# Steps that make the gather lists stand at other places in TensorE's work on x's chunks

## The chip, the cores and the metric

The kernel runs on one core of one Trainium2 chip. The metric is the device time of an execution in microseconds (us); lower is better. A core has five engines with a queue each: PE (TensorE, matmuls), DVE (VectorE), ACT (ScalarE), POOL (GpSimd) and SP (SyncE, which only issues DMAs here). Each works through its own instructions in the order of the program; they wait for each other on semaphores.

## The reference

`x` is 8 x 2048 x 128, `adj` a sparse 2048 x 2048 matrix (each entry is drawn with probability 0.002, made symmetric, and the diagonal is always there). Two layers follow each other:

```python
# layer 0
sj = inputs @ w_j
si = inputs @ w_i
res = si[:, :, None] + sj[:, None, :] + relation[None] * w_r + g_b
agg = jnp.einsum('bij,bjd->bid', res, inputs)
x = _layernorm(x + agg @ weight + bias, axis=-1)
# layer 1, A1 = A2 = adj
x1 = jnp.einsum('bnf,nw->bwf', x0, A)
x2 = 2.0 * jnp.einsum('bnf,nw->bwf', x1, A) - x0
out = jax.nn.relu(concat([X, x1, x2, x1, x2]) @ Theta1 + bias)
x = _layernorm(x + out, axis=-1)
```

The dense terms of layer 0 (si, sj) are of low rank. What costs is the product with `adj`, once in layer 0 and in two hops in layer 1.

## The kernel before, in words

The 2048 rows are 16 chunks of 128; a row of all eight batches has 1024 numbers. Four target chunks of layer 0 (0 to 3) are multiplied densely with adj's transposed columns. The other twelve, and both hops, use lists: for a strip of 32, 64 or 128 columns of `adj` the kernel finds the rows that have a nonzero there, gathers the adj entries of these rows and the rows of y (or u) by indirect DMAs from POOL's queue, and multiplies the small blocks.

The work before layer 0 runs in three stages.

1. `R_ORDER` loop: the chunks of `adj` are loaded and transposed, DVE reduces them to masks (which strip has a nonzero in which row), and the first eight chunks of x are done on the way. The transposed chunks are stored to `rr_d`, later joined there by copies of adj's columns (twelve DMAs of 1 MB on SP, `copies`).
2. The loop `for n in range(NX, NC)` over the remaining eight chunks of x (block n below). A block has eight transposes (`x_t`, PE, into banks 6 and 7, copied by ACT), the projections y = x W with si and sj (`y_of`, PE into banks 4 and 5, copied by ACT), and the dense pairs: `full_rows(0, acc0, ...)` and `full_rows(1, acc1, ...)`, two matmuls of 128x512 each (four instructions a pair in the trace), for target chunks 0 and 1. Between these stand the steps that make the lists, called by `lists_at`.
3. The code after the loop, written out by hand: more rounds for the lists, jobs, column sums, the dense target chunks 0 to 3, and then a loop over chunks 4 to 15 of layer 0.

The list chain goes through PE, ACT and DVE in turns. It makes first the lists of the 32-wide strips ("T"), then those of the halves ("H": 64- and 128-wide strips, which take the columns that are shared).

- `ranked`: a matmul with a triangle of ones into bank 6 ranks the rows of a column; DVE marks the first 64 in `et`.
- `candidates`: 14 transposing matmuls of `et` into banks 6 and 7, copied to `cand` by ACT. Then eight `round_of` on DVE: `max` takes the eight largest, `match_replace` strikes them out.
- `lists_end(0)`: turns the T lists (matmuls into bank 6, six DVE operations) into row numbers `idx`, `idr` and the flag `has`.
- `encode2`, `split2`, `candidates2`: the same for the halves: DVE encodes into `e2`, PE ranks into bank 7, DVE splits, PE transposes nine blocks into banks 6 and 7, ACT copies to `cand2`.
- `rounds2([r])`: round r of eight on `cand2` (96 x 1152). `lists_end(1)`, after the rounds, gives idx, idr and has for the halves.

A job fetches adj entries: `get_job` issues four (T) or three (H) indirect DMAs from `rr_d` into one of four slots of `st`; `keep_job` (DVE) multiplies what came with `has` and puts it into `rct` and `rc`, which frees the slot. `next_job` is a keep_job and a get_job. There are 24 jobs. `get_direct` gathers the adj entries of chunks 0 to 3 directly (28 DMAs). `get_rows` gathers rows of y.

The engines' instructions are kept in the order of the calls (class `Tied`), but the indirect DMAs of POOL's queue are placed by the scheduler: some gathers stand earlier than the calls do. Before, the queue has eight jobs (32 gathers), the memset of `rc`, six direct gathers, two y gathers (into `ring` and `trp`), and then direct gathers, jobs and y gathers mixed. The first gather of rows for chunk 4 into `Y` is the 93rd gather of the queue.

Before the loop's end nothing of DVE is between `split2` and `rounds2([0])`. After `rounds2([0])` comes a memset of banks 4 and 5, and then the first `next_job`.

```python
    rounds2([0])
    for b in bank[4:6]:
        dve.memset(b, 0.0)
    next_job()
    rounds2([1, 2])
    next_job()
```

All recorded operations have the line of a helper (L74), so that groups and instructions are told apart by the tiles.

Of the kernel before, what the change touches and what calls it, by code (L numbers as in the profile page):

```python
# [11 lines left out]
ALU = mybir.AluOpType  # L12
AX = mybir.AxisListType
# [5 lines left out]
def kernel(  # L19
# [44 lines left out]
    X_ORDER = list(range(ND, NC)) + list(range(ND))  # L64
# [11 lines left out]
    pe, dve, act = Tied(nc.tensor), Tied(nc.vector), Tied(nc.scalar)  # L76
# [47 lines left out]
    def load_later_constants():  # L124
        for i in range(4):
            sp.dma_start(out=b0row[:, i, :], in_=bias0[None, :])
        sp.dma_start(out=b1bc[:, 0, :], in_=bias1[None, :].to_broadcast([P, D]))
        sp.dma_start(out=th, in_=theta.rearrange("(m p) f -> p m f", p=P))
# [61 lines left out]
    both = st[:, 2 * NC * NT + 512:2 * NC * NT + 768].rearrange("p (c w) -> p c w", w=NC)  # L190
# [7 lines left out]
    def at_of(c):  # L198
        t = at4[:, c] if c < ND else ats[(c - ND) % len(ats)]
        return t.rearrange("p (j i) -> p j i", i=P)  # L200
# [17 lines left out]
    def load_x(c, t):  # L218
        sp.dma_start(out=t, in_=x[:, c * P:(c + 1) * P, :].rearrange("b p f -> p b f"))
        return t  # L220

    def copies(cs):
        for c in cs:
            sp.dma_start(out=rr_d[c - ND][:, 1, :], in_=adj[:, c * P:(c + 1) * P])
# [4 lines left out]
    def pump():  # L229
        while todo:  # L230
            what, n = todo[0]
            if what == "a" and n < done["a"] + 3:
                for w in (slice(0, N // 2), slice(N // 2, N)):
                    sp.dma_start(
                        out=am[n % 3][:, w], in_=adj[R_ORDER[n] * P:(R_ORDER[n] + 1) * P, w]
                    )
            elif what == "x" and n < done["x"] + 6:
                c = X_ORDER[n]
                xin[c] = load_x(c, ring[:, X_SLOT[n % 6]])
                if c < ND:  # L240
                    zs[c] = xin[c]
            elif what == "k":
                load_later_constants()
            elif what == "s" and done["a"] == NC:
                store_rt(n)
            elif what == "c" and done["a"] == NC:
                copies([n])
            else:
                return
            todo.pop(0)  # L250
# [31 lines left out]
    def store_rt(c):  # L282
        sp.dma_start(out=rr_d[c - ND][:, 0, :].rearrange("(j p) i -> p j i", p=P), in_=at_of(c))
# [11 lines left out]
    def y_of(n, xt):  # L295
        for b in range(0, B, 2):
            py = bank[4 + b // 2 % 2][:, 0:2 * (D + 2)].rearrange("p (i f) -> p i f", i=2)
            for i in range(2):
                pe.matmul(py[:, i, :], xt[b // HB][:, (b + i) % HB, :], wx, start=True, stop=True)
            act.copy(Y[:, X_ORDER[n], b:b + 2, :], py[:, :, 0:D])  # L300
            act.copy(sraw[:, X_ORDER[n], b:b + 2, :], py[:, :, D:D + 2])
# [14 lines left out]
    def half(c, h):  # L316
        return Y[:, c, h * HB:(h + 1) * HB, :].rearrange("p b f -> p (b f)")
# [13 lines left out]
    def full_rows(c, accs, js):  # L331
        at = at_of(c)
        for j in js:
            for h in range(2):
                pe.matmul(
                    accs[h], at[:, j, :], half(j, h), start=(j == js_first[c]), stop=False,
                    skip_group_check=True,
                )
# [3 lines left out]
    def acc_pair():  # L342
        par[0] ^= 1
        return bank[2 * par[0]:2 * par[0] + 2]

    acc0, acc1 = acc_pair(), acc_pair()
# [21 lines left out]
    def thetas():  # L368
        dve.tensor_add(th[:, 4, :], th[:, 2, :], th[:, 4, :])
        dve.tensor_sub(th[:, 2, :], th[:, 0, :], th[:, 4, :])  # L370
        dve.tensor_add(th[:, 0, :], th[:, 4, :], th[:, 4, :])
        dve.tensor_add(th[:, 1, :], th[:, 1, :], th[:, 3, :])
# [18 lines left out]
    miss = const.tile([P, 3], F32)  # L391
# [27 lines left out]
    def ranked():  # L419

        b = bank[6][:, 0:2 * NT].rearrange("p (r t) -> p r t", r=2)
        pe.matmul(b, lt, sums, start=True, stop=True)
        before = b
        for c in range(LR):
            dve.tensor_add(etr[:, :, c, :], before, mt[:, :, c, :])
            before = etr[:, :, c, :]
        dve.scalar_tensor_tensor(et, et, 64.0, NS_[:, 0:LT, :], op0=ALU.is_le, op1=ALU.mult)
# [5 lines left out]
    def encode2():  # L433
        dve.tensor_sub(NS_[:, 0:LT, :], NS_[:, 0:LT, :], et)
        nsp = NS_.rearrange("p c (w i) -> p c w i", i=2)
        dve.tensor_mul(pr, pr, num[:, :, None].to_broadcast([P, NC, 2 * NC]))
        dve.tensor_add(pr, pr, nsp[:, :, :, 0])
        for to, c in (
            (e2[:, 0:LR, 0:HC], slice(0, LR)), (vm, slice(LT, NC)),
            (e2[:, NP - LR:, HC:], slice(LR, LT)),  # L440
        ):
            n = c.stop - c.start
            dve.tensor_add(to[:, :, 0:32], pr[:, c, :], nsp[:, c, :, 1])
            dve.tensor_mul(
                to[:, :, 32:HC], both[:, c, :], num[:, c, None].to_broadcast([P, n, NC])
            )
        dve.tensor_scalar(mm, vm, 0.0, None, op0=ALU.is_gt)
        dve.tensor_scalar(m2, e2[:, 0:LR, 0:HC], 0.0, None, op0=ALU.is_gt)
        dve.tensor_reduce(ms[:, 0, :], m2.rearrange("p c l -> p l c"), AX.X, ALU.add)
        dve.tensor_add(ms[:, 1, :], ms[:, 0, :], mm[:, 0, :])  # L450
# [8 lines left out]
    def candidates():  # L459
        for g in range(0, LR, 4):  # L460
            b = by4(bank[6 + g // 4])
            n = min(4, LR - g)
            for i in range(n):
                for r in range(2):
                    pe.matmul(
                        b[64 * r:64 * r + 64, i, :], et[:, r * LR + g + i, :], ident, start=True,
                        stop=True, skip_group_check=True, tile_position=(0, 64 * r),
                    )
            act.copy(cand[:, g * P:(g + n) * P].rearrange("p (i f) -> p i f", f=P), b[:, 0:n, :])
# [14 lines left out]
    def round_of(to, of, r):  # L484
        dve.max(to[:, 8 * r:8 * r + 8], of)
        if r < 7:
            dve.match_replace(of, to[:, 8 * r:8 * r + 8], of, 0.0)
# [47 lines left out]
    def gather(to, src, ids, n, rows):  # L535
        pool.indirect_dma_start(
            out=to, out_offset=None, in_=src,
            in_offset=bass.IndirectOffsetOnAxis(ap=ids[:, n:n + 1], axis=0),
            bounds_check=rows - 1, oob_is_err=False,
        )  # L540

    def columns(c, what):
        if what == "T":
            return [QT * c + t for t in range(QT)]
        return [NT + 2 * c, NT + 2 * c + 1, NT + 2 * NC + c]
# [7 lines left out]
    def staged(k):  # L553
        return st[:, k % 4 * BD:]

    def get_job():
        what, c = jobs[got[0]]
        s = staged(got[0])
        got[0] += 1
        for n, i in enumerate(columns(c, what)):  # L560
            gather(
                s[:, n * 2 * P:(n + 1) * 2 * P], rr_d[c - ND].rearrange("n m f -> n (m f)"), idx, i,
                N,
            )
# [148 lines left out]
    def rounds2(rs):  # L713
        for r in rs:
            round_of(lists2[0:96], cand2[0:96], r)

    def next_job():
        keep_job()
        get_job()


    def lists_at(n):
        if n == 9:
            ranked()
        if n == 10:
            candidates()
            for r in range(8):
                round_of(lists, cand, r)
            dve.tensor_reduce(miss[:, 1:2], both, AX.XY, ALU.add)
            thetas()  # L730
        if n == 13:
            lists_end(0)
            get_job()
            get_job()
            encode2()
            get_job()
            get_job()
        if n == 14:
            split2()
        if n == 15:  # L740
            candidates2()

    for n in range(NX, NC):
        xt = x_t(n)
        pump()
        y_of(n, xt)
        lists_at(n)
        for c, acc in enumerate((acc0, acc1)):
            full_rows(c, acc, [X_ORDER[n - 1]])
        if n % 4 == 0:  # L750
            s_rows(X_ORDER[n - 4])
        if n == 9:
            s_rows(X_ORDER[0])
# [80 lines left out]
        load_own(0, y0_d, c, Y[:, c] if c < 12 else ring[:, 3 + c % 2], c < 12)  # L834


    rounds2([0])
    for b in bank[4:6]:
        dve.memset(b, 0.0)
    next_job()  # L840
    rounds2([1, 2])
    next_job()
    for c0 in range(0, NC, 4):
        column_sums(c0)
    make_ub()
    rounds2([3, 4])
    next_job()
    si_t(0)
    si_t(1)
# [327 lines left out]
```

## Time and profile before

| | us |
|---|---|
| median of 3 runs | 826.9 |
| lowest and highest of them | 826.63, 828.11 |
| the profiled execution, whole | 869.73 |
| its span, first to last instruction | 867.5 |
| PE busy | 734.0 (85%) |
| POOL busy | 444.1 (51%) |
| DVE busy | 396.4 (46%) |
| ACT busy | 195.0 (22%) |

The profile is of one execution, which took longer than the timed ones; its mean granted TensorE clock is 0.940 of full speed. Times in the profile count from the span's start. A line of the timeline has the start, the duration, the engine, the operation with the tile that it writes and those that it reads, and in brackets how long the engine idled before it and what ended that. A POOL line DMA_INDIRECT is one gather. In the profile `y_d` stands also for `y0_d`, buffer numbers being left out.

### The profile page before, as it was taken

The page shows a single profiled execution, that of the slowest core. Times are in us where ns is not written, and L with a number is a line of the kernel's source. Part 1 is how long each engine was busy: PE and PEld are TensorE (multiplying, and loading weights), DVE is VectorE, ACT ScalarE, POOL GpSimd, SP SyncE. Part 2 cuts the span into 40 slices and gives each one's busy share as a digit, 9 for nine tenths or more (in the row PEclk, how much of TensorE's full clock was granted, in tenths as well). Part 3 has the DMA queues.
Part 4 walks back from the last instruction along what each step waited for, and adds up shares of the span by engine and source line. Part 5 has one row for each costly group of instructions (what it writes and reads, how often), then busy time and mean ns, then how long its engine had stood idle before and what let it go on. Part 6 is the DMA issues. An engine that isn't in the chain of part 4 may idle for free.

```text
span 867.5 us, 10065 instructions
## 1 busy us (share of the span) xinstructions
PE 734.0 (85%) x3534; PEld 369.1 (43%) x3534; DVE 396.4 (46%) x603; ACT 195.0 (22%) x440; POOL 444.1 (51%) x433
## 2 busy tenths in 40 slices
PE   5988999679830869879999889999999889999993
PEld 4665666524420323434444534334343344444441
DVE  6675758093500506547664300000000267777775
ACT  5675544212310002223333200000000011111111
POOL 1000001556777574766662556665665567777640
PEclk9999999797975798889999999999999999999997
DMA  8999999992233455898997989999999689999982
GB/s 308 291 326 332 294 306 298 359 379 60 87 110 98 133 162 166 278 358 316 380 371 265 376 289 359 370 359 359 354 364 349 217 304 343 348 377 386 389 284 62
DMA packets 167059, 250.87 MB, mean 289 GB/s; under 512 B 17480, under 2 KB 118557, under 8 KB 167000
## 3 DMA queue, kind: packets, MB, share of 16 engines
q0 software_dynamic: 49280, 145.59, 47.1%
q1 hardware_dynamic: 95736, 79.31, 29.1%
q10 hardware_dynamic: 21984, 25.24, 8.2%
q8 instruction: 30, 0.49, 0.2%
q14 instruction: 29, 0.24, 0.1%
HBM read 231.67 MB, written 58.72 MB: 335 GB/s over the span
## 4 chain that ended last, share of the span: by engine, by line
PE 53%; DMA 22%; issue 9%; ACT 6%; another core or an unknown queue 6%; POOL 2%; DVE 1%; POOLq 0%; ACTq 0%
PE bank L74 53%; DMA Y<-u_d,idx 11%; DMA Y<-y_d,idx 5%; ACT Y L74 2%; POOL Y L74 2%; DMA ring<-y_d,idx 2%; ACT trp L74 1%; ACT rct L74 1%; DMA trp<-y_d,idx 1%; DMA y_d<-st 1%; DMA ring<-in_x_dram 1%; DVE st L74 1%; DMA wr<-in_L_gnn_g_w_dram 1%; ACT at L74 1%
## 5 line engine op out<-in xcount | busy, mean ns | idle before, releaser
L74 POOL DMA_INDIRECT Y<-y_d,idx x170 | 185.0, 1088 | 105.4 <-PE bank L74 51.4
L74 PE MATMUL bank<-Y,rc 128*32 128x512 f32 (+2 forms) x896 | 220.1, 609 | 20.0 <-DMA Y<-u_d,idx 9.0
L74 POOL DMA_INDIRECT st<-rr_d,idx x84 | 85.8, 1021 | 189.6 <-DVE rown L74 144.4
L74 POOL DMA_INDIRECT Y<-u_d,idx x112 | 111.6, 997 | 82.9 <-issue 45.1
L74 PEld LDWEIGHTS bank<-Y,rc 128*32 128x32 f32 (+2 forms) x896 | 58.0, 128 | 178.0 <-issue 121.3
L74 PE MATMUL bank<-Y,at 128*128 128x512 f32 x256 | 116.5, 606 | 0.0
L74 DVE TENSOR_REDUCE s<-sq 128x4 f32<-128x512 f32 x60 | 41.1, 686 | 71.8 <-ACT sq L74 47.3
L74 PEld LDWEIGHTS bank<-Y,at 128*128 128x128 f32 x256 | 48.3, 195 | 54.0 <-issue 53.8
L74 PE MATMUL bank<-th,at 128*128 128x128 f32 x384 | 52.3, 291 | 14.3 <-issue 14.1
L74 DVE COPY ring<-bank 128x512 f32<-128x512 f32 x10 | 6.9, 692 | 115.3 <-PE bank L74 74.9
L74 PEld LDWEIGHTS bank<-th,at 128*128 128x128 f32 x384 | 48.7, 203 | 20.1 <-issue 19.7
L74 PE MATMUL bank<-ident,rc 128*128 128x128 f32 (+2 forms) x302 | 46.1, 302 | 12.1 <-DMA rc<-in_adj_dram 6.4
L74 ACT COPY ring<-bank 128x512 f32<-128x512 f32 (+1 forms) x36 | 20.8, 585 | 156.2 <-PE bank L74 90.0
L74 PE MATMUL bank<-ub,sit 5*128 5x512 f32 x16 | 8.4, 1053 | 49.0 <-ACT sit L74 40.6
L74 DVE TENSOR_REDUCE st<-rc 128x64 f32<-128x2048 f32 x16 | 36.5, 2282 | 24.7 <-DMA rc<-in_adj_dram 24.7
L74 PE MATMUL bank<-wx,trp 128*128 128x130 f32 x256 | 37.6, 290 | 10.7 <-ACT sraw L74 5.0
L74 PE MATMUL bank<-Y,rct 128*32 128x512 f32 (+1 forms) x232 | 45.8, 607 | 0.7 <-DMA Y<-y_d,idx 0.6
L74 PEld LDWEIGHTS bank<-ident,rc 128*128 128x128 f32 (+2 forms) x302 | 34.9, 155 | 25.2 <-issue 9.5
L74 PE MATMUL bank<-ring,rd 128*128 128x512 f32 x92 | 43.5, 594 | 1.2 <-issue 1.2
L74 ACT ACTIVATE sq<-ring 128x512 f32<-128x512 f32 x26 | 16.4, 630 | 121.1 <-DVE ring L74 96.5
L74 PEld LDWEIGHTS bank<-wx,trp 128*128 128x128 f32 x256 | 31.9, 194 | 16.0 <-ACT sraw L74 8.4
L74 ACT COPY trp<-bank 128x512 f32<-128x512 f32 (+1 forms) x38 | 21.2, 586 | 62.0 <-PE bank L74 59.6
(173 smaller groups left out, 890.7 us busy)
## 6 DMA issues: line engine op xcount, KB each, us to landing
rc<-in_adj_dram SPq DMA_DIRECT2D x32, 512.0 KB
rr_d<-in_adj_dram SPq DMA_DIRECT2D x12, 1024.0 KB
ring<-in_x_dram SPq DMA_DIRECT2D x16, 512.0 KB
rr_d<-Y SPq DMA_DIRECT2D x8, 1024.0 KB
y_d<-Y SPq DMA_DIRECT2D x16, 512.0 KB
u_d<-ring ACTq DMA_DIRECT2D x12, 512.0 KB
ring<-u_d SPq DMA_DIRECT2D x10, 512.0 KB
y_d<-ring ACTq DMA_DIRECT2D x10, 512.0 KB
```

The costliest lines, as they stand in the source:

```text
L74: return lambda *a, **k: tc.keep_in_program_order(f(*a, **k))
```

## The change

`lists_at` gets a second argument and is called three times in a block: ahead of the projections (step 0), between them and the first dense pair (step 1), and between the two pairs (step 2). The steps move so:

- `ranked`: from block 9 after the projections to block 9 before them.
- `candidates` and its eight rounds: from block 10 after the projections to block 9 between the pairs.
- `lists_end(0)`, four jobs and `encode2`: from block 13 after the projections to block 12 after them. The reduction of `both` into `miss` and `thetas` (five small DVE operations) move from behind the eight rounds to behind `encode2`.
- `split2`: from block 14 to block 13, after the projections.
- `candidates2`: from block 15 after the projections to block 13 between the pairs.
- Round 0 of the halves' lists stands in block 14, rounds 1 and 2 in block 15. After the loop, round 3 stands between the first two jobs and round 4 before the third; rounds 5 to 7 stay.

In the built program every engine has the same instructions as before. On POOL ten 32-wide direct gathers that stood behind the first two y gathers (some behind the ninth to eleventh job) now stand before them, sixteen in a row after the memset of `rc`. SP's order is the same.

```diff
--- before.py
+++ after.py
@@ -719,34 +719,40 @@
         get_job()
 
 
-    def lists_at(n):
-        if n == 9:
+    def lists_at(n, step):
+        if (n, step) == (9, 0):
             ranked()
-        if n == 10:
+        if (n, step) == (9, 2):
             candidates()
             for r in range(8):
                 round_of(lists, cand, r)
-            dve.tensor_reduce(miss[:, 1:2], both, AX.XY, ALU.add)
-            thetas()
-        if n == 13:
+        if (n, step) == (12, 1):
             lists_end(0)
             get_job()
             get_job()
             encode2()
+            dve.tensor_reduce(miss[:, 1:2], both, AX.XY, ALU.add)
             get_job()
             get_job()
-        if n == 14:
+            thetas()
+        if (n, step) == (13, 1):
             split2()
-        if n == 15:
+        if (n, step) == (13, 2):
             candidates2()
 
     for n in range(NX, NC):
         xt = x_t(n)
         pump()
+        lists_at(n, 0)
         y_of(n, xt)
-        lists_at(n)
-        for c, acc in enumerate((acc0, acc1)):
-            full_rows(c, acc, [X_ORDER[n - 1]])
+        lists_at(n, 1)
+        full_rows(0, acc0, [X_ORDER[n - 1]])
+        lists_at(n, 2)
+        full_rows(1, acc1, [X_ORDER[n - 1]])
+        if n == 14:
+            rounds2([0])
+        if n == 15:
+            rounds2([1, 2])
         if n % 4 == 0:
             s_rows(X_ORDER[n - 4])
         if n == 9:
@@ -834,16 +840,15 @@
         load_own(0, y0_d, c, Y[:, c] if c < 12 else ring[:, 3 + c % 2], c < 12)
 
 
-    rounds2([0])
     for b in bank[4:6]:
         dve.memset(b, 0.0)
     next_job()
-    rounds2([1, 2])
+    rounds2([3])
     next_job()
     for c0 in range(0, NC, 4):
         column_sums(c0)
     make_ub()
-    rounds2([3, 4])
+    rounds2([4])
     next_job()
     si_t(0)
     si_t(1)
```

## The prediction

> **What bounds the kernel now.** I read the cores view, the page's 40 slices, the chain of waits, the windows, then the timelines of GpSimd (POOL), VectorE (DVE) and TensorE (PE) around the change. Slices first:
>
> ```profile
> PE   5988999679830869879999889999999889999993
> POOL 1000001556777574766662556665665567777640
> PEclk9999999797975798889999999999999999999997
> DMA  8999999992233455898997989999999689999982
> ```
>
> One digit is 21.7 us. PE and DMA are full up to about 190 us. From 200 to 290 us DMA is nearly empty and PE has a hole (digits 8, 3, 0), while POOL works. The hole is this:
>
> ```profile
> 240.66 5.64 another core or an unknown queue
> 246.90 10.04 another core or an unknown queue
> 257.91 27.09 another core or an unknown queue
> ```
>
> These chain lines are waits of ScalarE (ACT) for PE results that the program issues long before; together 42.8 us. The windows view gives a granted clock of 1.00 in 98:158, of 0.62 in 235:286. The profiled execution took 869.73 us (span 867.5, 2.2 around it), 42.8 more than the median of 826.9. So I take the hole as PE losing its clock in this execution only, and reckon for a "clean" run: 869.73 - 42.8 = 826.9. The profile also lost some time at 158-171 and 187-195 (8.2 and 3.2 us by the same kind of wait and by late PE starts), at 236 (3.0) and 318 (8.4); with the hole 65.6 us up to 330, of which only 42.8 reach the end: something else catches up. That is POOL:
>
> ```profile
> 147.67 1.15 POOL L74 DMA_INDIRECT st<-rr_d,idx  x1 [144.44 <-DVE rown L74]
> 167.63 1.00 POOL L74 DMA_INDIRECT st<-rr_d,idx  x1 [0.31 <-issue]
> 177.79 1.00 POOL L74 DMA_INDIRECT st<-rr_d,idx  x1 [9.16 <-DVE rc L74]
> 183.75 1.00 POOL L74 DMA_INDIRECT st<-rr_d,idx  x1 [1.07 <-DVE rc L74]
> 212.52 1.00 POOL L74 DMA_INDIRECT ring<-y_d,idx  x1 [2.75 <-issue]
> 294.26 1.00 POOL L74 DMA_INDIRECT Y<-y_d,idx  x1 [0.31 <-issue]
> ```
>
> One queue issues every gather at one per 1.30 us, in a fixed order. Before layer 1 it has 84 of rr_d (24 jobs), 28 direct and 84 of y rows: 196 x 1.30 = 255 us from 147.67, i.e. to 403 without a pause. Chunk 4, the first one that needs gathers, has its first at place 93 of the queue (294.26 in this profile). Clean, POOL reaches it at 273.6 (below), but PE, at chunk 4 at 328.63 in the profile, would be there at 328.63 - 65.6 = 263. So in a clean run PE waits for POOL at chunk 4. After it a chunk costs POOL 10 x 1.30 = 13.0 us while jobs remain (7 gathers and a job of 3), PE 10.5 (395.73 to 406.25); then gathers fill DMA (windows, 395:475, share 0.93). A POOL queue that runs earlier as a whole brings the end of layer 0 forward.
>
> What holds the queue's start is the list chain on DVE:
>
> ```profile
> 125.57 1.09 DVE L74 MAX8 lists<-rc 128x8 f32<-128x896 f32 x1 [5.70 <-ACT rc L74]
> 146.54 0.23 DVE L74 TENSOR_SCALAR has<-bank 128x64 f32<-128x64 f32 x1 [2.29 <-PE bank L74]
> 173.20 1.36 DVE L74 MAX8 lists<-rc 96x8 f32<-96x1152 f32 x1 [18.30 <-ACT rc L74]
> 176.12 1.03 DVE L74 MEMSET bank<- 128x512 f32 x2
> ```
>
> DVE idles 5.70, 2.29 and 18.30 us because the PE step it needs stands a chunk late in PE's order.
>
> **What the skill says.** "Perfetto Trace Analysis", section "DMA Instruction — SWDGE (GPSIMD)": a POOL DMA's profiled end is the last descriptor, not the landing. The trace agrees: the last gather of a job ends at 242.61 and the step that reads it starts at 244.55, so I add 1.9 us for landing. "TensorE: Matmul & The Clock Gate", section "Architectural detail: the array is 16× 32×32, not 1× 128×128": ACT and DVE queues are strict FIFO, GpSimd's per core of it. The trace agrees: DVE stands 9.80 us before 244.55 with other work behind. Same page, "What's actually happening": an idle PE runs at half clock; "Seeing it yourself" adds that the gate has been seen stuck low for 50 us and more. The trace has 9.4 us of PE busy in 51 us (235:286), which fits but doesn't prove it.
>
> **The change part by part.** The built order has the same instructions on every engine, so nothing is added or removed; only places move.
>
> *candidates, ranked: block 10 to block 9.* An x block is 7.0 us of PE (112.49 to 119.66 with ranked in it). Block 9 starts at 112.49. ranked now sits in the gap after its transposes; DVE needs 3.3 us (116.49 to 119.86) for it, while PE does the projections (2.3) and one pair (1.8): no stall. candidates starts at 118.3 instead of 123.26, DVE's rounds 2.31 later (123.26 to 125.57) at 120.6, and the eight rounds of 17.3 us end at 137.9, not 142.89.
>
> *lists_end(0): after the projections of block 12.* PE is there at 139.1. This is an added wait on DVE; behind it stand both dense pairs. Round eight is over 1.2 us before, so it costs nothing; if the rounds were later, PE would lose the difference. From its PE start to the first gather is 1.58 us (146.09 to 147.67): POOL starts at 140.7, 7.0 earlier. The copies of rr_d that these gathers read stand 8 us or more ahead: SP issues d6 to 121.6, d9 to 132.3, and a load issued to 87.7 had landed by 93.6 (6 us), while POOL wants d9 at 156. Sixteen gathers (20.8) run to 161.5.
>
> *miss and thetas moved behind encode2.* 1.5 us of DVE (142.80 to 144.25) now stand between encode2 and split2's DVE part. encode2 ends 7.0 after lists_end (146.09 to 153.09), at 146.1, when PE reaches split2 (146.3); DVE is through with the rest at 148.3. candidates2, after one pair, starts at 148.9: covered by 0.6 us; without that cover PE loses what is missing.
>
> *candidates2: block 15 to 13, three rounds in x.* From its PE start to round one is 4.98 us (168.22 to 173.20): 153.9; three rounds of 2.83 end at 162.4. But the first keep_job stands in DVE behind the memset of banks 4 and 5, which waits for block 15's projections, and these come behind candidates2's 4.3 us now: 153.2 + 1.8 + 7.0 + 3.6 = 165.6, ACT 0.4, memset 1.0, keep 0.4, 0.2 to POOL: 167.6. POOL has idled 6.1. Before, clean: block 15 at 157.32, candidates2 at 160.9, round one 165.9, POOL 4.59 later (173.20 to 177.79) at 170.5. Gain here 2.9.
>
> *The next jobs.* Before, two rounds stand between jobs: period 5.96 (177.79, 183.75), the fourth ends at 170.5 + 3 x 5.96 + 5.2 = 193.6. After, one round each (2.83 + 0.4 below 5.2), later two rounds with lead in hand: POOL is never stopped, 167.6 + 20.8 = 188.4. **Gain 5.2 us.**
>
> *What the scheduler moves on POOL.* Ten more direct gathers (32 wide) now stand ahead of the first y gather and of jobs 8 to 10; up to place 93 the count is the same, 2.0 us for the memset and 60 gathers: 273.6 before, 268.4 after. Jobs 8 to 10 come later: job 10 at 188.4 + 2.0 + 38 x 1.30 = 239.8, before 193.6 + 2.0 + 28 x 1.30 = 232.0. DVE's keep_job for it, and z_add of chunk 2 behind it, is 7.8 us later, at 247; the layernorm behind needs until 262, wanted by PE after chunk 4's last gather, about 284. SP moves nothing; the y stores wait for block 15 (166) as fourth in their queue, issued from 162.22, so at most 1 us. PE has the same work and its lists weren't waited for.
>
> **Sum.** 826.9 - 5.2 = 821.7 us (869.73 - 42.8 - 5.2 by the profiled execution). Bounds of what the trace doesn't show: if block 15 doesn't hold the memset, the whole 7.0; if before also loses the 2.75 at 212.52, 5.2 + 2.8 = 8.0; below, nothing. I take 5.2, since the clean order has lists_end(1) ready by 201, POOL there at 203.4.
>
> **Rivals.** *Larger*: the 2.75 us wait is real in timed runs: 826.9 - 8.0 = 818.9. For: the profile shows it; against: PE was 11.4 us late there. *No gain*: PE or DMA, not POOL, sets layer 0; for: the profile's PE is late at chunk 4, and DMA is full in the tail; against: of the 65.6 us that PE lost, 22.8 were caught up, which a layer set by PE couldn't do. Time 826.9. *Slower*: jobs 8 to 10 behind ten direct gathers hold DVE, z_add and layernorm of chunk 2, and so PE: 826.9 + 7.8 = 834.7. It decides once that layernorm ends later than 284; it has 22 us.
>
> **Chances.** Forecast 0.61, larger 0.15, no gain 0.15, slower 0.09. Faster by over 0.2% (1.7 us, about what a measurement can tell from no change): 0.76; within: 0.15; slower: 0.09. The range goes from 816.5 (gain 8.0 and a shorter tail) to 826.5; half of no gain and all of slower are outside, and a little below. The forecast's own range is 819 to 824.
>
> **What would show it.** First gather near 140.7; the fifth job near 167.6 and a DVE releaser before it; the next three without pause; rounds for the halves from 154. Wrong if PE idles before lists_end(0) or candidates2, or if POOL waits for PE or DVE between 190 and 268.

## The result, and the profile after

| | us |
|---|---|
| change, median of 22 runs | 823.12 (819.36 to 827.69) |
| before, median of 22 runs | 827.1 (824.13 to 830.51) |
| ratio | 0.9947, 95% interval 0.9931 to 0.9962 |
| the profiled execution of the change, whole | 820.96 |
| its span | 819.0 |
| PE, POOL, DVE, ACT busy in it | 732.9, 447.1, 398.0, 195.5 |

By the ratio the change is 4.4 us faster (3.1 to 5.7 by the interval); the forecast was 5.2. A ratio here is an estimate with its interval and not exactly the quotient of the two medians, which is 0.9952 (4.0 us). In some groups of runs every kernel, that of before too, took 847 to 894 us with a mean granted TensorE clock of 0.92 to 0.95 instead of 0.96 to 0.98, and such times are only compared with each other.

The 40 slices of the page after (one digit is 20.5 us):

```profile
PE   6999999999996569999998899999999999999993
POOL 1000001677777777766625476655664777776730
PEclk9999999999997789999999999999999999999997
DMA  9999999995535678999989899999997899999971
```

PE's hole of the profile before is gone; the digits 6, 5, 6 at 246 to 307 us are waits for ACT and for gathers, shown below. POOL is evenly busy from 143 us on. The timeline of POOL, at the places of the lines shown before:

```profile
139.49 1.15 POOL L74 DMA_INDIRECT st<-rr_d,idx  x1 [136.26 <-DVE rown L74]
159.48 1.00 POOL L74 DMA_INDIRECT st<-rr_d,idx  x1 [0.31 <-issue]
163.72 1.00 POOL L74 DMA_INDIRECT st<-rr_d,idx  x1 [3.23 <-DVE rc L74]
208.07 1.00 POOL L74 DMA_INDIRECT ring<-y_d,idx  x1 [0.31 <-issue]
267.31 0.99 POOL L74 DMA_INDIRECT Y<-y_d,idx  x1 [0.30 <-issue]
```

The first gather, the sixteenth, the fifth job, the first y gather and the 93rd gather, the first one of rows for chunk 4. One pause is left in the queue, 3.23 us ahead of the fifth job; the 76 gathers that follow it up to the last of these lines have at most 0.31 us of idle time ahead of them. DVE, the same steps as before the change:

```profile
119.05 1.09 DVE L74 MAX8 lists<-rc 128x8 f32<-128x896 f32 x1 [2.67 <-ACT rc L74]
138.36 0.23 DVE L74 TENSOR_SCALAR has<-bank 128x64 f32<-128x64 f32 x1 [1.99 <-PE bank L74]
150.11 1.36 DVE L74 MAX8 lists<-rc 96x8 f32<-96x1152 f32 x1 [3.34 <-ACT rc L74]
162.04 1.02 DVE L74 MEMSET bank<- 128x512 f32 x2 [3.44 <-ACT sraw L74]
```

The wait ahead of the first round of the halves has gone from 18.30 to 3.34 us. What holds the fifth job is now the memset: it waits 3.44 us for ACT's last copy of block 15's projections (`sraw`), and the keep_job stands behind it. PE at the end of the dense chunk 3 (`sit` is a small transposed copy of si, made by ACT) and at chunks 4 and 5:

```profile
258.45 2.35 PE L74 MATMUL bank<-ub,sit 5*128 5x512 f32 x4 [6.22 <-ACT sit L74]
260.73 3.78 PE L74 MATMUL bank<-Y,rd 128*128 128x512 f32 x4
271.95 1.88 PE L74 MATMUL bank<-Y,rct 128*32 128x512 f32 x2 [7.44 <-DMA Y<-y_d,idx]
...
302.74 1.97 PE L74 MATMUL bank<-Y,rct 128*64 128x512 f32 x2 [7.43 <-DMA Y<-y_d,idx]
```

PE begins chunk 4 at 260.73 with its own rows (`rd`), is through with them at 264.5 and waits 7.44 us for the gather that POOL issued at 267.31. In chunk 5 it waits 7.43 us once more. The same place in the profile before:

```profile
328.63 3.78 PE L74 MATMUL bank<-Y,rd 128*128 128x512 f32 x4
332.34 4.10 PE L74 MATMUL bank<-Y,rct 128*32 128x512 f32 x24
```

There PE comes late, with a granted clock of 0.58 in 240 to 290 us, and doesn't wait. So that profile could not show the wait on POOL's queue.

### The profile page after: what moved, and what is told of

It reads as the page before. It is cut to its first block, busy times and chain, and to the rows that moved or that the text cites. A ratio compares the mean times of both kernels' runs of the same rounds, so it can differ in the third digit from the quotient of the medians.

```text
span 819.0 us, 10068 instructions
## 1 busy us (share of the span) xinstructions
PE 732.9 (89%) x3534; PEld 364.1 (44%) x3534; DVE 398.0 (49%) x603; ACT 195.5 (24%) x440; POOL 447.1 (55%) x433
## 4 chain that ended last, share of the span: by engine, by line
PE 37%; DMA 33%; issue 13%; ACT 7%; POOL 5%; DVE 4%; POOLq 0%; ACTq 0%; DVEq 0%
PE bank L74 37%; DMA Y<-u_d,idx 17%; DMA Y<-y_d,idx 5%; DMA st<-rr_d,idx 4%; DMA ring<-y_d,idx 3%; ACT Y L74 2%; POOL st L74 2%; POOL Y L74 2%; DMA rc<-in_adj_dram,idr 1%; ACT rct L74 1%; DVE s L74 1%; ACT at L74 1%; ACT trp L74 1%; DVE st L74 1%; DMA y_d<-st 1%
## 5 line engine op out<-in xcount | busy, mean ns | idle before, releaser
L74 POOL DMA_INDIRECT Y<-y_d,idx x170 | 189.7, 1116 | 81.9 <-PE bank L74 36.3
L74 PE MATMUL bank<-Y,at 128*128 128x512 f32 x256 | 114.0, 594 | 0.0
L74 PE MATMUL bank<-Y,rct 128*32 128x512 f32 (+1 forms) x232 | 61.2, 637 | 21.0 <-DMA Y<-y_d,idx 21.0
L74 PE MATMUL bank<-ident,rc 128*128 128x128 f32 (+2 forms) x302 | 44.3, 293 | 11.6 <-DMA rc<-in_adj_dram 6.5
L74 PE MATMUL bank<-th,at 128*128 128x128 f32 x384 | 47.9, 277 | 1.9 <-ACT at L74 1.9
L74 PEld LDWEIGHTS bank<-th,at 128*128 128x128 f32 x384 | 45.2, 192 | 7.0 <-ACT at L74 3.8
L74 PEld LDWEIGHTS bank<-ident,rc 128*128 128x128 f32 (+2 forms) x302 | 33.1, 148 | 25.7 <-issue 9.9
L74 PEld LDWEIGHTS bank<-Y,rct 128*32 128x32 f32 (+1 forms) x232 | 13.9, 123 | 64.6 <-DMA Y<-y_d,idx 34.4
L74 ACT COPY Y<-bank 128x256 f32<-128x256 f32 (+1 forms) x72 | 27.8, 398 | 30.9 <-PE bank L74 30.6
```

The lines of the kernel that those rows point to most:

```text
L74: return lambda *a, **k: tc.keep_in_program_order(f(*a, **k))
```

## Experiments

**Theory.** POOL's one queue of gathers, 1.30 us each, sets when layer 0 ends; the change pays because the queue is earlier and has fewer pauses. **Rival.** PE or DMA sets layer 0, and the gain comes from the PE waits in x; gathers more or less are then hidden. The traces leave few such waits to save: before the change PE waits at most 0.41 us at a time between 95 and 160 us, and after it at most 0.29 us between 100 and 178 us.

**1. The change once more**, unchanged, beside the next two.

> The change itself, on the chip of these runs, as the mark for the two kernels beside it. Theory (POOL's queue sets the end of layer 0 where PE keeps its clock): 0.995 of before, with PE waiting for gathers in chunks 4 and 5. If the chip holds PE's clock down between 155 and 330 us, PE is late at chunk 4 instead and the gain is gone or reversed.

Measured: 822.82 us, ratio 0.9931 (0.9903 to 0.9958), before 826.98 in this group. The gain is there again, 4.2 us by the medians and 5.7 by the ratio.

**2. Eight gathers more in POOL's queue.** Their results are read by nobody; nothing is left out.

```diff
+    spare8 = const.tile([P, 8, TW], F32)
+
+    def get_more():
+        for t in range(8):
+            gather(spare8[:, t, :], adj.rearrange("n (c f) -> (n c) f", f=TW), idr, t, N * NT)
...
     rounds2([7])
     acc2 = bank[4:6]
+    get_more()
     full_rows(2, acc2, LAST[:2])
```

> The change, with eight more gathers of adj (32 wide, into a spare tile that nothing reads) in POOL's queue behind its first sixteen. They move 131 KB. POOL has a pause of 3.2 us there, so 8 x 1.30 - 3.2 = 7.2 us remain. Theory (POOL's queue sets the end of layer 0): 7.2 us slower than the change, about 830 where the change has 823. Rival (PE or DMA sets it): no slower than the change by more than 1 us.

The call stands further down, but the scheduler puts the eight gathers behind the first sixteen. Measured: 831.33 us, ratio 1.0053 (1.0035 to 1.0072), by the medians 8.5 us more than the change, by the ratios 10.1. POOL's timeline:

```profile
159.44 1.00 POOL L74 DMA_INDIRECT st<-rr_d,idx  x1 [0.30 <-issue]
160.75 1.00 POOL L74 DMA_INDIRECT spare<-in_adj_dram,idr  x1 [0.30 <-issue]
...
169.86 1.00 POOL L74 DMA_INDIRECT spare<-in_adj_dram,idr  x1 [0.30 <-issue]
171.16 1.00 POOL L74 DMA_INDIRECT st<-rr_d,idx  x1 [0.30 <-DMA y_d<-Y]
...
274.58 1.00 POOL L74 DMA_INDIRECT Y<-y_d,idx  x1 [0.30 <-PE bank L74]
```

The eight stand where the pause was: 8 x 1.30 = 10.4 us of queue, of which 3.2 fill the pause, 7.2 net. The 93rd of the old gathers comes at 274.58 instead of 267.31, 7.3 later. PE:

```profile
268.32 2.35 PE L74 MATMUL bank<-ub,sit 5*128 5x512 f32 x4 [13.34 <-ACT sit L74]
280.55 6.82 PE L74 MATMUL bank<-Y,rct 128*32 128x512 f32 x18 [6.22 <-DMA Y<-y_d,idx]
```

The later jobs also hold DVE longer, so that PE's wait for `sit` grows from 6.22 to 13.34 us; but behind it PE still waits 6.22 us for rows, and this wait ends last. A change of nothing but the queue is paid in full, and a little over. This speaks for the theory and against the rival; DMA, at a share of 0.44 between 190 and 267 us of the change, is far from full there.

**3. 28 gathers out of the queue before layer 0.** The direct gathers are held back until the first hop: they take their row numbers from a copy that DVE makes in chunk 13.

```diff
+    idd = const.tile([P, NI], I32)
...
-                rc[:, at:at + w], adj.rearrange("n (c f) -> (n c) f", f=w), idr, i, N * (N // w)
+                rc[:, at:at + w], adj.rearrange("n (c f) -> (n c) f", f=w), idd, i, N * (N // w)
...
-        get_direct(1 if c < 10 else 2 if c < 12 else 3)
+        if c == NC - 3:
+            dve.tensor_copy(idd, idr)
...
-                get_direct(1)
+                get_direct(3)
```

> The change, with all 28 direct gathers held back (their row numbers are copied by DVE in chunk 13 of layer 0) until the turn to hop 1 and hop 1 itself, where the rows of chunks 0 to 3 are first read. Theory: 28 x 1.30 = 36 us less in POOL's queue before chunk 4, of which PE's own arrival at chunk 4 (255) leaves about 15 at chunk 4 and 24 at chunk 5; the hop may give some back, as its own queue gets longer: 15 to 30 us faster than the change, 793 to 808 where the change has 823. Rival (PE or DMA sets layer 0): as the change, or slower by the gathers in the hop.

Measured: 804.92 us, ratio 0.9712 (0.9671 to 0.9753), 18 us less than the change. 28 x 1.30 = 36.4 us of gathers left the stage. Chunk 4 doesn't wait for rows any more; of PE's two long waits one is left, that of chunk 5:

```profile
255.16 1.40 PE L74 MATMUL bank<-ub,sit 5*128 5x512 f32 x4 [0.35 <-ACT sit L74]
256.49 1.98 PE L74 MATMUL bank<-Y,rd 128*128 128x512 f32 x4
258.40 3.79 PE L74 MATMUL bank<-Y,rct 128*32 128x512 f32 x24
...
278.40 4.94 PE L74 MATMUL bank<-Y,rct 128*64 128x512 f32 x8 [7.36 <-DMA Y<-y_d,idx]
```

POOL had three longer pauses here: 3.26 us ahead of the fifth job, 8.83 ahead of the first y gather, 2.35 after it.

**4. The memset behind the first keep_job.** In the change, the first `next_job` goes ahead of the memset of banks 4 and 5, so that it doesn't wait for block 15.

```diff
+    next_job()
     for b in bank[4:6]:
         dve.memset(b, 0.0)
-    next_job()
     rounds2([3])
```

> The change with the first keep_job and get_job ahead of the memset of banks 4 and 5, so that the job doesn't wait for the projections of block 15. Theory: the 3.2 us pause ahead of the fifth job goes, the 93rd gather comes 3.2 us earlier, and the kernel takes some 3 us less than the change, 819.6 us, ratio 0.991 to the kernel before. Rival (the pause is hidden behind something else): 822.8 us as the change, ratio 0.995.

Measured: 820.37 us, ratio 0.9913 (0.9893 to 0.9933), before 828.25 in this group: 2.75 us less than the change's 823.12. The change itself was not run in this group. By the ratios of its two groups (0.9947, 0.9931) the difference is 2.8 or 1.5 us, and the intervals overlap: the run agrees with the theory's 3 us, but doesn't exclude the rival. The thirty-two gathers of the eight jobs now follow each other (the pause is 0.3 us).

**5. Pauses out of experiment 3.** The kernel of 3 with the order of 4, and with `rounds2([5, 6])`, a job, `rounds2([7])` and `lists_end(1)` ahead of `rank9(0, acc0)`, since the profile of 3 names a DVE step at the end of `lists_end(1)` as what released the first y gather.

> Layer 0 with GpSimd's queue relieved of the 28 direct gathers (held to the first hop), with the first job ahead of the memset of banks 4 and 5, and with lists_end(1) ahead of rank9, so that the first y gather doesn't wait for it. Theory (the queue sets the end of layer 0 as long as PE waits for y rows in chunks 4 and 5; in the kernel with the direct gathers held alone, 804.9 us, GpSimd waited 3.3, 8.8 and 2.4 us, and PE 7.4 us for rows of chunk 4): up to 12 us of pauses go, of which PE's wait of 7.4 can pay: 795 to 802 us. Rival (with the queue shorter by 36 us, DMA or PE sets the end): 804 to 806 us.

(The 7.4 us are PE's wait in chunk 5 shown above, not one in chunk 4.) Measured: 804.54 us, ratio 0.9723 (0.9701 to 0.9744). It can't be told from experiment 3. The rival's number came, but the run doesn't decide for the rival, because the queue did not become earlier: the pause ahead of the fifth job is gone (0.30 us), and the one ahead of the first y gather has grown by nearly as much. The first y gather of 3, and then that of 5:

```profile
195.62 1.00 POOL L74 DMA_INDIRECT ring<-y_d,idx  x1 [8.83 <-DVE miss L74]
```

```profile
196.30 1.00 POOL L74 DMA_INDIRECT ring<-y_d,idx  x1 [13.09 <-DVE rc L74]
```

`lists_end(1)` ends at 195.5 in the one and at 184.2 in the other, and the gathers start within 0.7 us. So `lists_end(1)`, the name in brackets in 3, was not all that held the gather: something else ends at about 195. The stores of y are the candidate. The windows of kernel 5:

```profile
core 0: us, PE busy (x) PEld busy (x) DVE busy (x) ACT busy (x) POOL busy (x), PEclk, DMA share, GB/s
167.00:194.00 27.00, 25.11 (x148) 10.14 (x147) 20.20 (x38) 9.85 (x19) 12.85 (x13) 0.87 0.99 394
194.00:196.00 2.00, 2.00 (x6) 0.85 (x5) 2.00 (x6) 0.00 (x0) 0.00 (x0) 1.00 0.06 23
```

DMA is full until 194 (share 0.99) and then empty (0.06), and the gather reads what the sixteen y stores have written. By the trace the last of them, issued at 184.4, lands 11.0 us later, at about 195.4; in 3 it is 184.2 and 10.7 us, about 194.9. Both are 0.7 to 0.9 us ahead of the gather. That the gather waits for their landing was not tried alone; the step named in brackets in 5, a keep_job that ends at 195.7, isn't ruled out either.

**The five kernels side by side.** The profiles' x stages start up to 3 us apart, so the times are counted from the first matmul of `candidates` (116.7 to 119.8). "Rows" is the first gather into `Y`, "hop" the first matmul of the first hop that reads gathered rows of u (`Y,rc`). The last column is against 823.12, across groups of runs.

| | rows | hop | median us | less than the change |
|---|---|---|---|---|
| eight gathers more | 157.9 | 333.1 | 831.3 | -8.2 |
| the change | 150.6 | 325.4 | 823.1 | |
| keep_job first | 148.5 | 322.6 | 820.4 | 2.7 |
| direct gathers held | 124.0 | 299.6 | 804.9 | 18.2 |
| the same, pauses out | 123.6 | 298.9 | 804.5 | 18.6 |

In the first three rows the start of the hop follows the gather about 1:1 (7.7 and 2.8 us for 7.3 and 2.1; two profiles of the change are 0.2 apart in the gather and 0.7 in the hop), and the time follows the hop. In the last two the gather is 27 us earlier and the hop 26, but only 18 reach the end: between 410 and 600 us PE waits for u rows 20.6 and 21.2 us, 13.0 in the change.

**6. One part of the change alone.** `t_only` has only the steps of the T lists moved and the halves' as before; its GpSimd order is that of before. `h_only` is the reverse, with the GpSimd order of the change; as its `lists_end(0)` stands in block 13, `split2` and `candidates2` stand in block 14, one block behind those of the change. The edit of `h_only` against the change:

```diff
-        if (n, step) == (9, 0):
+        if (n, step) == (9, 1):
             ranked()
-        if (n, step) == (9, 2):
+        if (n, step) == (10, 1):
             candidates()
...
-        if (n, step) == (12, 1):
+        if (n, step) == (13, 1):
             lists_end(0)
...
-        if (n, step) == (13, 1):
+        if (n, step) == (14, 1):
             split2()
-        if (n, step) == (13, 2):
+        if (n, step) == (14, 2):
             candidates2()
```

In the profiles of these runs, with the kernel of before as a control and the kernel of experiment 4 in another group, the mean granted clock is only 0.927 to 0.939.

> The kernel before, unchanged, for a trace without the low clock. Theory (POOL's queue sets the end of layer 0): no change, ratio 1.000 within 0.003. In its trace, with the 2.73 us that the transposes of the halves take at full clock, the fifth job starts near 168, the eighth ends near 191, and the first gather of rows into Y (the 93rd) is near 271; PE waits for it. Rival (PE or DMA sets layer 0): PE is at chunk 4 after its gathers have landed and doesn't wait for them.

> Only the part of the T lists is moved (ranked and candidates in block 9, lists_end(0), jobs and encode2 in block 12); split2 stays in block 14, candidates2 in block 15, and no round for the halves is in x. POOL's order is that of before. Theory (POOL's queue sets the end, and the fifth job its pace): the first gather is 7 us earlier, near 140, but the fifth job waits for the memset behind round 0 as before, so POOL only idles longer: no gain, ratio 1.000 (0.998 to 1.002). Rival (the queue's start is what counts): as the whole change, 0.995.

> Only the part of the halves is moved: the T lists as before, candidates2 in block 14 between the pairs instead of block 15, three rounds ahead of the memset, one round between the next jobs. POOL's order is that of the change. Theory: the first gather is as before (147), the fifth job about as before (168), but the next three jobs follow without the pauses of 0.76 us each: gain 2.3 us, ratio 0.997. Rival (the queue's start is what counts): no gain, 1.000.

> The change, with the first keep_job and get_job ahead of the memset of banks 4 and 5 instead of behind it. Theory: the memset, which waits for block 15's projections, holds the fifth job by 3.2 us; without it POOL has no pause and everything behind is 3.2 us earlier: 7.6 us below before, ratio 0.991. Rival (PE or DMA sets layer 0, POOL's earlier start gives no more): as the change, 0.995.

> The kernel before with the steps of the T lists moved as in the change (ranked, candidates, lists_end(0), the first four jobs and encode2 earlier); the halves' steps stay where they were (split2 in block 14, candidates2 in block 15, no round within x), and GpSimd's order is that of the kernel before. Theory (the end of layer 0 is set by the last pause of GpSimd's queue before the first y rows): the first gather comes some 7 us earlier, the pause ahead of the fifth job grows by as much, jobs 5 to 8 run as before, and nothing is gained: ratio 0.999 to 1.001 to the kernel before. Rival (the earlier start of the lists is what pays): ratio 0.995 as in the change.

> The change with the T lists' steps at their old places (ranked in block 9 and candidates in block 10 after the projections, lists_end(0) in block 13); the halves' steps are early (split2 in block 14 after the projections, candidates2 in block 14 between the pairs, rounds within x), with one round between jobs after the loop. Theory: the first gather stands at about 146, the first sixteen end at 167, the fifth job follows almost without a pause, and jobs 5 to 8 run back to back, some 3 us behind those of the change: ratio 0.997. Rival (the start of the lists pays): ratio 1.000. If the ten direct gathers ahead of the y gathers cost something, 1.000 too, and then the trace has GpSimd's eighth job earlier than in the kernel before without an earlier end.

> The same kernel as t_only once more, on another chip: the kernel before with only the T lists' steps early. Theory: its first gather comes some 7 us earlier than before, but the fifth job waits, as before, for candidates2 and the memset behind the projections of block 15, so the 93rd gather stands where it stood before (271 to 274 us) and the time is that of the kernel before, ratio 0.999 to 1.001. Rival (the earlier start of the queue pays, even with the longer pause): ratio 0.995, the 93rd gather at 269.

| | median us | before, same group | ratio (95%) |
|---|---|---|---|
| before_again | 870.94 | 871.78 | 1.0042 (0.9997 to 1.0086) |
| t_only | 863.57 | 871.78 | 0.9889 (0.9804 to 0.9974) |
| t_only_b | 864.62 | 866.65 | 0.9930 (0.9895 to 0.9964) |
| t_only_c | 859.02 | 862.89 | 1.0045 (1.0010 to 1.0079) |
| h_only | 887.26 | 871.78 | 1.0165 (1.0078 to 1.0252) |
| h_only_b | 880.06 | 866.65 | 1.0153 (1.0108 to 1.0198) |
| keep_first | 877.67 | 871.78 | 1.0082 (1.0048 to 1.0117) |

The theory's numbers fail here. By the ratios the first two runs of `t_only` (0.9974 and 0.9964 at most) and the third (1.0010 at least) exclude each other; the quotients of the medians are 0.991, 0.998 and 0.996. The rival's 0.995 for `t_only` lies inside the interval of the first two. `h_only` is slower, where the theory had 0.997 and the rival 1.000. And `keep_first`, 0.8% slower than before here, is 0.9% faster in experiment 4, with a clock of 0.97. As one and the same kernel changes its sign between the groups, these runs decide nothing on how the 4.4 us divide between the two parts: neither that the halves' part pays nor that the earlier start alone doesn't. That stays open.

Two things can be read in their traces. One is the pause ahead of the fifth job: in the three traces of `t_only` this job starts at 173.6 to 180.6, in the two of before at 177.8 and 181.3, and the pause ahead of it is 12.4 to 20.2 us instead of 9.2 and 12.8. The earlier first gather went into the pause, as the theory has it, though the clock from 155 to 190 us was 0.80 to 0.94 in these five. The other is where the first gather is, since up to 155 us the clock is 0.98 to 1.00 in all of them:

| lists_end(0) | profiles | first gather |
|---|---|---|
| block 13 (before, before_again, h_only, h_only_b) | 4 | 146.4 to 147.7 |
| block 12 (all others) | 10 | 139.0 to 144.1 |

Counted from the first matmul of `candidates`, it is 24.4 us in the first line and 22.7 in the second; the rest of the difference is that `candidates` itself stands earlier.

## Why the prediction was right, step by step

**What bounds the kernel: right, and the step that carried the rest.** POOL's queue was taken as the bound from a profile in which PE was the late one. Experiment 2 showed it by adding to the queue alone (8.5 us for 7.2) and experiment 3 by taking gathers out (18 us); experiment 4 points the same way. They show it for the kernel after the change. That it held before as well is inferred: the queue was later there, and PE had the same work. PE's arrival at chunk 4, reckoned at 263, was 260.73, and this is partly luck: the reckoning had taken PE's waits for `sit` out, and 6.22 us of such a wait are in the measured time, so that PE's work up to there was over-reckoned by 8.5 us.

**First gather: right.** 140.7 was forecast; 139.49 and 141.29 in the two profiles of the change, whose x stages start 1.8 us apart. `lists_end(0)` cost PE nothing: its matmuls at 137.91 have no wait ahead of them.

**Fifth job: the gate right, the size off.** The memset behind block 15's projections was named as what holds it, and it does. The time was 163.72 instead of 167.6 and the pause 3.2 instead of 6.1 us. `candidates2` started 1.5 us earlier than reckoned (147.38, not 148.9), about as much as the whole trace runs ahead. The rest is one term: `candidates2` was taken as 4.3 us of PE, and as 4.98 us from its PE start to round one, from these rows of the profile before:

```profile
168.22 3.62 PE L74 MATMUL bank<-ident,rc 128*96 128x128 f32 x16
172.26 0.60 PE L74 MATMUL bank<-ident,rc 128*96 128x128 f32 x2 [0.42 <-ACT rc L74]
```

After the change it is

```profile
147.38 2.17 PE L74 MATMUL bank<-ident,rc 128*96 128x128 f32 x18
```

The next matmuls start at 149.39, 2.0 us behind its start, and round one at 150.11, 2.73 us behind it. The rows of before lay in a stretch (168.2 to 172) with a granted clock of 0.50, that of after in one with 1.00. The prediction had taken that profile's lost time out of the totals, but had left this duration in. Since the same term stood in both the reckoning of before and that of after, it changed the difference little.

**Jobs 5 to 8 without a pause: right.** The seventeenth gather is at 163.72, the thirty-second at 183.52: 15 x 1.32.

**93rd gather: right at 268.4 (267.31 and 268.92), partly by two errors that cancel.** The eighth job ended 3.9 us earlier than forecast (184.5, not 188.4), but the memset and 60 gathers behind it took 82.8 us, not 80.0. Five starts between them stand 1.5 to 2.1 us apart instead of 1.30, which makes 2.8 us, and the second profile of the change has the same five; nothing shows what lengthened them.

**Gain: 5.2 forecast, 4.4 measured (3.1 to 5.7).** The difference is within the interval. How much later the 93rd gather of the kernel before is at the full clock was not seen: the two profiles of it have a mean clock of 0.940 and 0.938. So the sum's two parts (2.9 us at the fifth job, 2.3 from the pauses behind it) were not measured one by one.

**Rivals.** *No gain* is out by the ratio and by experiment 2. *Larger*: 8.0 us lies outside the interval. The argument against it was thinner than it looked: with 2.73 us for `candidates2` instead of 4.98 the queue of before would have come to its first y gather at 201.1 instead of 203.4, and lists_end(1) was reckoned ready by 201. *Slower*: its mechanism is there, at another place than was argued. The late jobs do hold DVE: at 251.77 a keep_job waits 6.04 us for its gather, and layernorm of chunk 2 behind it ends at 259.6 (262 was reckoned). Layernorm itself is in time, but ACT's copy of `sit` for chunk 3 stands behind the layernorm's `sq` steps in ACT's order, and PE waits for that copy, the 6.22 us at 258.45 shown above. The prediction asked only when the layernorm's own result was wanted (284), and not what else queues behind it. It cost nothing here because PE waits for rows behind it in any case; in experiment 3, where the jobs come early, the wait for `sit` is 0.35 us.

**Signs named ahead.** PE idles neither ahead of lists_end(0) nor ahead of candidates2, and POOL waits for neither PE nor DVE between 190 and 268.

## What to carry to other kernels

Where one in-order queue issues every gather, count its instructions, find the place of the first one that the next stage needs, and compare its time with PE's arrival: a pause ahead of that place can cost its length, unless a later wait of the queue takes it up (experiment 5), and the cheapest gain may be to move gathers that nobody needs yet behind it (18 us here, against 4.4 by starting the queue earlier). When a step is held late on an in-order engine, ask what else stands behind it there, not only who wants its result. And from a profile with a lowered clock take neither totals nor single durations without asking for the clock at that place.

## What the runs showed of the hardware beyond that

- A gather takes POOL 1.00 us and the next starts 0.30 later; the eight 32-wide ones of experiment 2, the 128x256 ones of the jobs and those of y's rows (1024 numbers each) have the same pitch of 1.30 us, but for single ones of 1.5 to 2.1 us.
- The lowered clock is no property of a chip: the same chip gave the kernel before 871.78 us in one group of runs and 826.98 in a later one. What set it was not found.
- From the end of a gather on POOL to the step that reads it, 1.9 us was taken in the prediction, from a job of `rr_d`. For the first rows of y it was 3.65 us (267.31 + 0.99 to 271.95).
